# Filler products in TensorE's foreseen stops, layer norms on GpSimd, later issues behind transfers, and new planning tables in a decoder layer

## The chip, the core and the metric

The kernel runs on one core of a Trainium2 chip. A core has five engines, each with its own queue of instructions: TensorE (PE in the profile; its weight loads are PEld), VectorE (DVE), ScalarE (ACT), GpSimd (POOL) and SyncE (SP), which issues the DMA transfers here. Engines wait for one another by semaphores. The metric is device time in microseconds: 1229.28 as the median of three runs of the kernel before (1228.77 to 1231.69).

## The reference

A decoder layer on x of shape (4, 1024, 256), fp32, with three residual blocks: causal self-attention with 16 heads of 16 channels, cross-attention to a context of 77 rows, and a gated feed-forward network with integer weights. Each block begins with a layer norm without weights:

```python
def _layernorm(x, axis=-1, eps=1e-05):
    m = jnp.mean(x, axis=axis, keepdims=True)
    v = jnp.var(x, axis=axis, keepdims=True)
    return (x - m) / jnp.sqrt(v + eps)

x = x + _L0_attn_ref(_layernorm(x), Wq, bq, Wk, bk, Wv, bv, Wo, bo, W_cross, shift_weights, gate)
x = x + _L0_xattn_ref(_layernorm(x), ctx, ctx, mask, xWq, xWk, xWv, xWo)
x = x + _L0_ffn_ref(_layernorm(x), w_gate, w_up, w_down)
```

In the self-attention the scores are `(gt * q W_cross k + (1 - gt) * q (M k)) / 4` with M built from `shift_weights`, then a causal softmax; both score terms are products of q with a mixed k, so their mixing can be folded into the projection weights. In the cross-attention `scores = where(masked, -1e9, scores)` before the softmax. The feed-forward block is `silu(x @ wg.T) * (x @ wu.T) @ wd.T` with 768 hidden channels and weights that are integers from -127 to 127 divided by 127.

## The kernel before

The rows are cut into eight chunks of 512, chunk (b, n) being half n of batch b; on chip a chunk is four tiles of 128 rows by 256 columns (QT = 4). Each chunk goes through these parts:

- `project` (L781): load x, layer norm, eight transposes to xnT, then the k, q and v projections. A projected q or k is split into a high and a low part (`spread`), and transfers (L738) spread the heads over partitions; the scores can start when these have landed.
- `maxima` (L838): scores once, query rows on partitions (L866, and L874 for the causal mask), whose row maxima VectorE takes out of PSUM (mt, L879). `shift` (L747) transposes them.
- `attend` (L907): scores again with keys on partitions (L949), minus the maxima by a product with the selection matrix `sel` (L955), the causal mask (L962), exp on ScalarE (L968) and the product with v (L992). Ahead of its first scores it loads x once more (L919) and GpSimd adds the output bias (L922). It ends with the quotients (L679) and `out_proj` (L698: product L717, addition to x on VectorE L722).
- `cross_attention` (L1052): layer norm, transposes, q projection (L766) and its spreading transfers, a mask product (L1106), scores for the maxima (L1114), their maxima (L1120), the scores again (L1160), exp (L1162), product with v (L1173), `out_proj`.
- `ffn` (L1182): stores x (L1200), layer norm, transposes, a high and a low part of the normalised rows (xh L1207, xl L1209), six hidden chunks of 128 (products L1229; tanh L1235, gating on VectorE L1237, hT L1239 on ScalarE and L1240 on GpSimd), the down products (L1263), the addition to x on VectorE (L1269) and the store (L1272).
- two further parts, `late_weights` and `load_ffn`, prepare the cross-attention's and the feed-forward's weights in the first part of the run. The first of them makes `sel` and `selB` and then sets the flag "selections".

A layer norm is `row_scales` (statistics of four tiles on VectorE, L153 and L154; variance plus epsilon, L156; its power -1/2 on GpSimd, L158; for cross-attention a factor per row, L160) and `normal_rows` (L163; four operations `(x - mean) * scale` of 128 x 256 on VectorE, L166). `layer_norm` calls both. There are 24 in all: 8 each for `project` (the tiles xr; the first chunk's is x00), `cross_attention` and `ffn` (the tiles xn).

**Who sets the order.** Each part is a Python generator. Before it writes instructions it yields a `piece`: the time that they will take on TensorE, the buffers that they take, the earliest start, and the times of what follows on other engines (`use`). All parts run as streams beside one another, and `weave` (L468) picks, while the kernel is built, the stream whose next piece can start first by the planner's own account of engines, buffers and transfers. To a stream's start it adds a number from the table LATES (L1290), one per stream and chunk, which lets a part go earlier or later than the account alone would. The outcome is a fixed order of TensorE's instructions; VectorE's is fixed in the same way up to the flag "begun", and after it the orders of the other engines follow from a scheduler that gives each engine its instructions by the order in which the data come. If the account has TensorE idle for over REST = 1.3 us (L496), it counts what follows for COLD = 5.0 us at a lower rate. These numbers only plan: what an instruction waits for are semaphores.

**Buffers.** PSUM tiles come from `pair()` (three of two banks) and `single()` (two of one bank), L82 to L89; SBUF tiles from rings: w4 (six, for x, xn, xnT, xh, xl), es (six), f2 (six), q, k, v, and x (three). A tile that is asked for waits for the last reader of the buffer that it gets.

Of the kernel before, what the change touches and what calls it, by code (L numbers as in the profile page):

```python
# [8 lines left out]
F32 = mybir.dt.float32  # L9
# [5 lines left out]
ALU = mybir.AluOpType  # L15
# [4 lines left out]
P = 128  # L20
# [7 lines left out]
def tile_decoder_layer(  # L28
# [25 lines left out]
    nc = tc.nc  # L54

    B, S, D = x.shape
# [6 lines left out]
    NG = H // 4  # L63
# [18 lines left out]
    pp = ctx.enter_context(tc.tile_pool(name="pp", bufs=3, space=PSUM))  # L82
    ps = ctx.enter_context(tc.tile_pool(name="ps", bufs=2, space=PSUM))

    def pair():
        return pp.tile([P, 2, CH], F32, tag="pair", name="pair")

    def single():
        return ps.tile([P, CH], F32, tag="single", name="single")  # L89


    ident = const.tile([P, P], F32, name="ident")
# [46 lines left out]
    def x_rows(b, n):  # L139
        xt = wide([P, QT, D], "xr")  # L140
        nc.sync.dma_start(xt, x[b, n * CH : (n + 1) * CH, :].rearrange("(t p) d -> p t d", p=P))
        return xt
# [17 lines left out]
            nc.gpsimd.tensor_tensor(rs, rs, keep, ALU.mult)  # L160
        return mv, rs

    def normal_rows(xt, mv, rs, xn=None):  # L163
        xn = xt if xn is None else xn
        for i in range(QT):
            nc.vector.tensor_scalar(  # L166
                xn[:, i, :], xt[:, i, :], mv[:, i, 0:1], rs[:, i : i + 1],
                ALU.subtract, ALU.mult,
            )
        return xn  # L170
# [133 lines left out]
    first = row_scales(x00)  # L304
    bvx = stage.tile([P, NC, P], F32, name="bvx")
    nc.vector.tensor_copy(bvx, bvn.unsqueeze(2).to_broadcast([P, NC, P]))
    normal_rows(x00, *first)

    def transposed(src, n, put):

# [150 lines left out]
    def piece(pe, use=(), at=0.0, cond=None, free=(), mode="whole", **take):  # L461

        return dict(pe=pe, use=use, at=at, cond=cond, free=free, mode=mode, take=take)

    def weave(*streams, until=None):
        while True:  # L468
            live = [s for s in streams if s.next is not None]
            if not live or until in flags:  # L470
                return
            can = []
            for s in live:
                p = s.next
                if p["cond"] is not None and not p["cond"]():
                    continue
                t = max(
                    tensor["end"], p["at"], *(slots[k].when(c) for k, c in p["take"].items()), 0.0
                )
                if p["pe"] and p["mode"] != tensor["mode"]:  # L480
                    t += SWITCH
                if p["use"] and p["take"]:

                    eng, us = p["use"][0]
                    t = max(t, busy[eng].start(t + p["pe"], us) - p["pe"] - 1.0)
                if t < 1.0e8:
                    can.append((t + (s.lates[s.chunk] if s.lates else 0.0), t, s))
            assert can, [s.next for s in live]
            soon = min(c[0] for c in can) + WAIT
            _, t, s = next(c for c in can if c[0] <= soon)  # L490
            p = s.next
            s.got = {k: [slots[k].take() for _ in range(c)] for k, c in p["take"].items()}
            s.end = t + p["pe"]
            if p["pe"]:
                if t - tensor["end"] > REST:
                    tensor["slow"] = t + COLD  # L496
                s.end += min(max(tensor["slow"] - t, 0.0) / 2, p["pe"])
                tensor.update(end=s.end, mode=p["mode"])
            for token in p["free"]:
                give(token, s.end)  # L500
            s.done = s.end
            for eng, us in p["use"]:
                s.done = busy[eng].run(s.done + LATE, us)
            s.next = next(s.pieces, None)
# [188 lines left out]

        return rest

    NORM = [("DVE", 2.6), ("POOL", 1.1), ("DVE", 1.7)]

    def out_proj(st, nat, t_nat, w, xt):  # L698

# [80 lines left out]
    def project(st, b, n):  # L780

        if (b, n) == (0, 0):
            yield piece(0.0, w4=1)
            xnT, t_x, at = x00T, st.got["w4"], 0.0
        else:
            yield piece(
                0.0, use=[("DMA", 4.0)] * (b > 0) + NORM, w4=1,
                cond=lambda: (("half", b - 1) if b else ("projected", 0, 0, 0)) in flags,
            )
            t_xn = st.got["w4"]  # L790
            xn = x01 if (b, n) == (0, 1) else x_rows(b, n)
            normal_rows(xn, *row_scales(xn))
            flags.add(("normal", b, n))
            yield piece(
                1.1, use=[("ACT", 1.05)], at=st.done + LATE, pair=1, w4=1, free=t_xn
            )
            xnT = transpose_rows(xn)
            st.release("pair")
            t_x = st.got["w4"]
            at = st.done + LATE  # L800
# [102 lines left out]
    def attend(st, b, n):  # L903
# [6 lines left out]
        for g in range(NG):  # L910
            c = g // 2
            if g % 2 == 0:
                yield piece(0.0, cond=lambda: (b, n, c) in shifts and (b, n) in vT and "selections" in flags)
                ms, at, t_ms = shifts.pop((b, n, c))
                if g == 0:
                    yield piece(0.0, x=1, use=[("DMA", 4.0)])
                    xt = xpool.tile([P, QT, D], F32, tag="x", name="x", bufs=3)
                    xs[b, n] = xt, st.got["x"][0]
                    nc.sync.dma_start(  # L919
                        xt, x[b, n * CH : (n + 1) * CH, :].rearrange("(t p) d -> p t d", p=P)  # L920
                    )
                    nc.gpsimd.tensor_tensor(  # L922
                        xt, xt, bo_b.unsqueeze(1).to_broadcast([P, QT, D]), ALU.add
                    )
                q, t_q, _ = qT.pop((b, n, c))
                over = [t_ms, t_q]
                if n == NQ - 1:
                    over += [kT[b, m, c][1] for m in range(NQ)]
            acc = []
            for kb in range(nk):  # L930
# [70 lines left out]
                lag.append(weigh)  # L1001
                if len(lag) > 1:
                    yield from lag.pop(0)()
                if tails and kb == 1:
                    nat, t_nat = yield from quotients(st, tails.pop(), nat, t_nat)
        yield from lag.pop()()
        nat, t_nat = yield from quotients(st, tails.pop(), nat, t_nat)
        yield from out_proj(st, nat, t_nat, woT, xt)
        flags.add(("attended", b, n))

    def quotients(st, tail, nat, t_nat):
        rest, toks, at, g = tail
        yield piece(
            0.55, use=[("DVE", 0.75)], at=at, single=1, free=toks,
            **({"w4": 1} if nat is None else {}),
        )
        if nat is None:
            nat, t_nat = wide([P, QT, D], "nat"), st.got["w4"][0]
        rest(nat, g)
        st.release("single")  # L1020
        return nat, t_nat
# [257 lines left out]
    def every(part, lates, chunks=range(NQ)):  # L1279
# [8 lines left out]
        return Stream(pieces, lates)  # L1288

    LATES = (  # L1290
        [0.00, 0.00, 0.00, 0.00, -0.03, 0.00, -0.31, 0.00],
        [0.00, 0.00, 0.00, 0.00, 0.00, 0.00, -0.23, 0.00],
        [0.00, 0.00, 0.00, 0.00, 0.00, 0.00, 0.00, 0.00],
        [-1.02, 0.03, 0.00, -0.48],
        [0.54, 0.47, 0.00, 0.31],
        [-0.20, -0.15, -0.42, -0.02, 0.00, 0.33, 0.00, 0.00],
    )
    streams = [
        every(maxima, LATES[0]), every(cross_attention, LATES[1]), every(attend, LATES[2]),
# [67 lines left out]
```

## Time and profile before

| what | before |
|---|---|
| median of three runs | 1229.28 us |
| the profiled execution | 1232.86 us |
| its span, first to last instruction | 1231.1 us |
| TensorE busy (mean granted clock) | 1110.8 us (0.958 of full) |
| VectorE busy | 729.9 us |
| ScalarE busy | 562.6 us |
| GpSimd busy | 130.8 us |
| transfers | 76.44 MB, mean 62 GB/s |

The span is counted from the first to the last instruction of one execution; some 1.8 us of that execution lie outside it. A line of the waits gives for TensorE's waiting instruction the engine and the line that released it, and then the total in us, the times, the longest. A line of the timeline gives the start in us, the busy time of a run of like instructions, engine, line, operation, what is written from what, the shape and the number of them, and in brackets how long the engine had been idle and who ended it. A line of the instruction groups gives the count, the busy time in us, the mean in ns, and the idle time of the engine before it. A busy TensorE is not one at full rate: the row PEclk tells the clock that was granted.

### The profile page before, as it was taken

To read this page: it belongs to the slowest core of one execution; us is meant where nothing else is said; L and a number is where in the kernel's file an instruction comes from. 1 tells how busy PE (TensorE), PEld (TensorE's weight loads), DVE (VectorE), ACT (ScalarE), POOL (GpSimd) and SP (SyncE) were. 2 spreads that over 40 slices of the span, in tenths; PEclk is the share of its full clock that TensorE was granted. 3 is DMA by queue.
4 is the path that set the end of the run, shared out by engine and by line. 5 is a ranking of instruction groups with operands and counts; after the bars stand their busy time and mean duration, and the time that the engine had idled before them with its cause. 6 is when DMAs were issued, how large, how long until landed. Compare 5 with 4: busy or idle time off the path is not lost. (4 is left out here: it accounts for less than half of the span.)

```text
span 1231.1 us, 22029 instructions
## 1 busy us (share of the span) xinstructions
PE 1110.8 (90%) x9059; PEld 684.9 (56%) x9059; DVE 729.9 (59%) x1247; ACT 562.6 (46%) x801; POOL 130.8 (11%) x138
## 2 busy tenths in 40 slices
PE   6679989999999898999898998999999889996875
PEld 4445544557555466557555456556575545565654
DVE  5566786354687856255777856347458666136342
ACT  3044544654434463753353563653535336661521
POOL 4031000002000012001100002000110000011212
PEclk9798999999999999999999998999999989998986
DMA  6992315537732016555533015444826140006000
GB/s 124 130 201 63 58 33 69 69 53 92 97 55 40 9 38 110 75 71 87 87 52 38 8 42 70 85 63 60 102 44 91 36 63 8 18 1 86 1 35 19
DMA packets 65438, 76.44 MB, mean 62 GB/s; under 512 B 22451, under 2 KB 39399, under 8 KB 65332
## 3 DMA queue, kind: packets, MB, share of 16 engines
q1 hardware_dynamic: 64227, 74.62, 39.1%
q8 instruction: 73, 1.20, 0.5%
q10 hardware_dynamic: 1104, 0.35, 0.1%
q14 instruction: 34, 0.27, 0.1%
HBM read 15.28 MB, written 9.33 MB: 20 GB/s over the span
## 5 line engine op out<-in xcount | busy, mean ns | idle before, releaser
L968 ACT ACTIVATE es<-pair 128x1024 f32<-128x1024 f32 (+3 forms) x384 | 300.8, 812 | 252.6 <-PE pair L962 178.4
L879 DVE TENSOR_REDUCE mt<-pair 128x2 f32<-128x1024 f32 (+3 forms) x384 | 351.4, 952 | 92.3 <-PE pair L874 60.8
L866 PE MATMUL pair<-k,q 64*128 64x512 f32 (+3 forms) x768 | 163.2, 428 | 29.8 <-DVE mt L879 12.6
L949 PE MATMUL pair<-q,k 64*128 64x512 f32 (+3 forms) x768 | 161.4, 417 | 22.4 <-DVE mt L879 16.5
L992 PE MATMUL single<-es,vs 128*32 128x512 f32 (+3 forms) x1536 | 166.2, 506 | 0.1
L866 PEld LDWEIGHTS pair<-k,q 64*128 64x128 f32 x768 | 76.0, 188 | 121.4 <-DVE mt L879 41.7
L955 PE MATMUL pair<-ms,sel 64*128 64x512 f32 (+3 forms) x768 | 134.6, 347 | 0.0
L949 PEld LDWEIGHTS pair<-q,k 64*128 64x128 f32 x768 | 73.2, 187 | 102.6 <-issue 34.8
L1240 POOL TENSOR_TENSOR hT<-h,hT 128x512 fp32r<-128x512 f32 x48 | 61.4, 1280 | 306.8 <-ACT hT L1239 297.2
L1162 ACT ACTIVATE es<-pair 77x1024 f32<-77x1024 f32 x64 | 63.4, 1020 | 45.8 <-PE pair L1160 45.5
L955 PEld LDWEIGHTS pair<-ms,sel 64*128 64x128 f32 x768 | 74.2, 190 | 3.1
L1120 DVE TENSOR_REDUCE mx<-pair 128x8 f32<-128x616 f32 x64 | 48.7, 794 | 43.7 <-PE pair L1114 43.7
L1263 PE MATMUL pair<-wdT,hT 128*128 128x256 f32 x384 | 63.3, 320 | 11.6 <-POOL hT L1240 4.8
L158 POOL TENSOR_TENSOR rs<-ve,mhalf 128x4 f32<-128x4 f32 x24 | 24.3, 1012 | 439.5 <-DVE ve L156 439.4
L1235 ACT ACTIVATE h<-pair 128x512 f32<-128x512 f32 x48 | 28.7, 598 | 89.0 <-PE pair L1229 84.8
L874 PE MATMUL pair<-cm_qk,id 64*128 64x64 bf16 (+1 forms) x1024 | 69.0, 211 | 0.0
L962 PE MATMUL pair<-cm_kq,id 64*128 64x64 bf16 (+1 forms) x1024 | 67.3, 211 | 0.0
L1236 DVE SCALAR_TENSOR_TENSOR h<-h,pair 128x512 f32<-128x512 f32 x48 | 33.0, 687 | 57.5 <-ACT h L1235 57.2
L1263 PEld LDWEIGHTS pair<-wdT,hT 128*128 128x128 f32 x384 | 55.8, 216 | 18.4 <-POOL hT L1240 6.3
L1114 PE MATMUL pair<-k2s,q 128*128 128x156 f32 x256 | 46.7, 308 | 12.1 <-DMA q<-hi 5.3
L992 PEld LDWEIGHTS single<-es,vs 128*32 128x32 f32 x1536 | 32.4, 109 | 40.7 <-issue 29.6
L674 ACT COPY aS<-single 128x512 f32<-128x512 f32 x64 | 37.5, 589 | 31.6 <-PE single L992 19.0
(180 smaller groups left out, 1575.0 us busy)
## 6 DMA issues: line engine op xcount, KB each, us to landing
q<-hi SPq DMA_DIRECT2D x128, 128.0 KB, 5.1
q<-lo SPq DMA_DIRECT2D x128, 128.0 KB, 6.3
k<-hi SPq DMA_DIRECT2D x64, 128.0 KB, 4.3
k<-lo SPq DMA_DIRECT2D x64, 128.0 KB, 6.0
xr<-in_x_dram SPq DMA_DIRECT2D x8, 512.0 KB, 6.0
x<-in_x_dram SPq DMA_DIRECT2D x8, 512.0 KB, 7.4
x_dram<-x SPq DMA_DIRECT2D x8, 512.0 KB, 2.6
out_dram<-x SPq DMA_DIRECT2D x8, 512.0 KB, 3.7
```

The lines of the kernel that those rows point to most:

```text
L866: nc.tensor.matmul(t[:, j, :w], q[r, a, i * P : (i + 1) * P], k[r, a, :w], start=True, stop=True,)
L874: nc.tensor.matmul(t[:, j, w - P + 64 * half : w], id2[r, half], cm_qk[r, half, 64 * half :], start=False, stop=True, skip_group_check=True,)
L879: nc.vector.tensor_reduce(mt[:, i, :, p, kc], t[:, :, :w], AX.X, ALU.max)
L949: nc.tensor.matmul(t[:, j, lo:], k[r, a, ki * P : (ki + 1) * P], q[r, a, lo:], start=True, stop=False,)
L955: nc.tensor.matmul(t[:, j, lo:], sel[r, hp, :], ms[r, lo:], start=False, stop=True)
L962: nc.tensor.matmul(t[:, j, lo : lo + 64 * (half + 1)], id2[r, half], cm_kq[r, half, : 64 * (half + 1)], start=False, stop=True, skip_group ...
L968: nc.scalar.activation(es[:, :, lo:], t[:, :, lo:], AF.Exp)
L992: nc.tensor.matmul(acc[0][W * jj : W * (jj + 1), lo:], vs[:, ki, V1 * h : V1 * h + W], both[jj // 2][:, jj % 2, lo:], start=(kb == 0), sto ...
L1120: nc.vector.tensor_reduce(mt[:, i, h4 : h4 + 4, :].rearrange("q (k p) j -> q k (p j)", k=2), tv[:, :, :, :S2], AX.X, ALU.max,)
L1162: nc.scalar.activation(es[:S2], t[:S2], AF.Exp)
L1240: nc.gpsimd.tensor_tensor(hs[:, 1, :], h, hs[:, 0, :].bitcast(F32), ALU.subtract)
L1263: nc.tensor.matmul(t[:, i, :], h[1][:, v, i * P : (i + 1) * P], w[:, h[0], :], start=(m == 0), stop=(m == len(terms) - 1),)
```

## The change

1. *Filler products.* In `weave`, where a piece of TensorE would start over REST after the last one ended, and a PSUM buffer for it is free early, and `sel` exists, the idle time less 0.7 us is noted (`stand`). The next `pair()` or `single()` then first writes so many products of 512 columns (one per 0.235 us of it) into the tile that it hands out, from `selB` and `sel`. Nothing reads what they write: the products that follow begin with `start=True`. Where fillers are noted the planner doesn't count the slow rate.
2. *Norms on GpSimd.* `normal_rows` runs on GpSimd, but for the first chunk's x00. The planner's price of a norm (`NORM`) becomes 2.4 us of VectorE and then 3.4 of GpSimd.
3. *Later issues.* In `project` the load of x has a piece of its own, and the norm's instructions are issued in a second piece whose earliest start is the load's end by the account. In `attend` the load of x moves from ahead of the first scores to the last group's first block, and GpSimd's addition of the bias to a piece behind the last product with v. The account prices either transfer at 6.5 us (4.0 before).
4. *Tables.* The six rows of LATES (maxima, cross-attention, attend, project of the first and of the second half of a batch, ffn) have new entries.

```diff
--- before.py
+++ after.py
@@ -82,11 +82,23 @@
     pp = ctx.enter_context(tc.tile_pool(name="pp", bufs=3, space=PSUM))
     ps = ctx.enter_context(tc.tile_pool(name="ps", bufs=2, space=PSUM))
 
+
+
+    stand = {"us": 0.0}
+
+    def stirred(t, part):
+        for _ in range(int(stand["us"] / 0.235)):
+            nc.tensor.matmul(part, selB, sel[:, 0:4, :], start=True, stop=True)
+        stand["us"] = 0.0
+        return t
+
     def pair():
-        return pp.tile([P, 2, CH], F32, tag="pair", name="pair")
+        t = pp.tile([P, 2, CH], F32, tag="pair", name="pair")
+        return stirred(t, t[:, 0, :])
 
     def single():
-        return ps.tile([P, CH], F32, tag="single", name="single")
+        t = ps.tile([P, CH], F32, tag="single", name="single")
+        return stirred(t, t)
 
 
     ident = const.tile([P, P], F32, name="ident")
@@ -160,10 +172,10 @@
             nc.gpsimd.tensor_tensor(rs, rs, keep, ALU.mult)
         return mv, rs
 
-    def normal_rows(xt, mv, rs, xn=None):
+    def normal_rows(xt, mv, rs, xn=None, eng=nc.gpsimd):
         xn = xt if xn is None else xn
         for i in range(QT):
-            nc.vector.tensor_scalar(
+            eng.tensor_scalar(
                 xn[:, i, :], xt[:, i, :], mv[:, i, 0:1], rs[:, i : i + 1],
                 ALU.subtract, ALU.mult,
             )
@@ -304,7 +316,7 @@
     first = row_scales(x00)
     bvx = stage.tile([P, NC, P], F32, name="bvx")
     nc.vector.tensor_copy(bvx, bvn.unsqueeze(2).to_broadcast([P, NC, P]))
-    normal_rows(x00, *first)
+    normal_rows(x00, *first, eng=nc.vector)
 
     def transposed(src, n, put):
 
@@ -492,7 +504,11 @@
             s.got = {k: [slots[k].take() for _ in range(c)] for k, c in p["take"].items()}
             s.end = t + p["pe"]
             if p["pe"]:
-                if t - tensor["end"] > REST:
+                idle = t - tensor["end"]
+                early = max([slots[k].when(1) for k in ("pair", "single") if k in p["take"]] or [t])
+                if idle > REST and early < tensor["end"] + 0.5 and "selections" in flags:
+                    stand["us"] = idle - 0.7
+                elif idle > REST:
                     tensor["slow"] = t + COLD
                 s.end += min(max(tensor["slow"] - t, 0.0) / 2, p["pe"])
                 tensor.update(end=s.end, mode=p["mode"])
@@ -693,7 +709,7 @@
 
         return rest
 
-    NORM = [("DVE", 2.6), ("POOL", 1.1), ("DVE", 1.7)]
+    NORM = [("DVE", 2.4), ("POOL", 3.4)]
 
     def out_proj(st, nat, t_nat, w, xt):
 
@@ -784,11 +800,12 @@
             xnT, t_x, at = x00T, st.got["w4"], 0.0
         else:
             yield piece(
-                0.0, use=[("DMA", 4.0)] * (b > 0) + NORM, w4=1,
+                0.0, use=[("DMA", 6.5)] * (b > 0), w4=1,
                 cond=lambda: (("half", b - 1) if b else ("projected", 0, 0, 0)) in flags,
             )
             t_xn = st.got["w4"]
-            xn = x01 if (b, n) == (0, 1) else x_rows(b, n)
+            xn = x_rows(b, n) if b else x01
+            yield piece(0.0, use=NORM, at=st.done)
             normal_rows(xn, *row_scales(xn))
             flags.add(("normal", b, n))
             yield piece(
@@ -912,16 +929,6 @@
             if g % 2 == 0:
                 yield piece(0.0, cond=lambda: (b, n, c) in shifts and (b, n) in vT and "selections" in flags)
                 ms, at, t_ms = shifts.pop((b, n, c))
-                if g == 0:
-                    yield piece(0.0, x=1, use=[("DMA", 4.0)])
-                    xt = xpool.tile([P, QT, D], F32, tag="x", name="x", bufs=3)
-                    xs[b, n] = xt, st.got["x"][0]
-                    nc.sync.dma_start(
-                        xt, x[b, n * CH : (n + 1) * CH, :].rearrange("(t p) d -> p t d", p=P)
-                    )
-                    nc.gpsimd.tensor_tensor(
-                        xt, xt, bo_b.unsqueeze(1).to_broadcast([P, QT, D]), ALU.add
-                    )
                 q, t_q, _ = qT.pop((b, n, c))
                 over = [t_ms, t_q]
                 if n == NQ - 1:
@@ -1001,9 +1008,19 @@
                 lag.append(weigh)
                 if len(lag) > 1:
                     yield from lag.pop(0)()
+                if g == NG - 1 and kb == 0:
+                    yield piece(0.0, x=1, use=[("DMA", 6.5)])
+                    xt = xpool.tile([P, QT, D], F32, tag="x", name="x", bufs=3)
+                    xs[b, n] = xt, st.got["x"][0]
+                    nc.sync.dma_start(
+                        xt, x[b, n * CH : (n + 1) * CH, :].rearrange("(t p) d -> p t d", p=P)
+                    )
+                    x_at = st.done
                 if tails and kb == 1:
                     nat, t_nat = yield from quotients(st, tails.pop(), nat, t_nat)
         yield from lag.pop()()
+        yield piece(0.0, use=[("POOL", 1.5)], at=x_at)
+        nc.gpsimd.tensor_tensor(xt, xt, bo_b.unsqueeze(1).to_broadcast([P, QT, D]), ALU.add)
         nat, t_nat = yield from quotients(st, tails.pop(), nat, t_nat)
         yield from out_proj(st, nat, t_nat, woT, xt)
         flags.add(("attended", b, n))
@@ -1288,12 +1305,12 @@
         return Stream(pieces, lates)
 
     LATES = (
-        [0.00, 0.00, 0.00, 0.00, -0.03, 0.00, -0.31, 0.00],
-        [0.00, 0.00, 0.00, 0.00, 0.00, 0.00, -0.23, 0.00],
         [0.00, 0.00, 0.00, 0.00, 0.00, 0.00, 0.00, 0.00],
-        [-1.02, 0.03, 0.00, -0.48],
-        [0.54, 0.47, 0.00, 0.31],
-        [-0.20, -0.15, -0.42, -0.02, 0.00, 0.33, 0.00, 0.00],
+        [0.00, -0.03, -0.10, 0.00, 0.00, -0.04, 0.01, -0.57],
+        [0.02, 0.00, 0.00, 0.00, 0.03, 0.00, 0.00, 0.00],
+        [0.43, -0.03, 0.06, -0.10],
+        [0.61, 0.21, 0.14, 0.21],
+        [0.00, -0.30, 0.00, -0.14, 0.08, 0.32, -0.26, 3.69],
     )
     streams = [
         every(maxima, LATES[0]), every(cross_attention, LATES[1]), every(attend, LATES[2]),
```

## The prediction

> **What bounds the kernel now.** I began with the page's slices of the span: the busy tenths of TensorE and the tenths of full clock that it was granted, 31 us a digit.
>
> ```profile
> PE   6679989999999898999898998999999889996875
> PEclk9798999999999999999999998999999989998986
> ```
>
> TensorE is the bound: busy 1110.8 of 1231.1 us, VectorE 729.9, ScalarE 562.6, GpSimd 130.8. Its 120.3 us of idleness lie in the first 60 us (some 25), in the tail from 1110 us (about 34) and in scattered stops between (about 57). Clock digits under 9 stand in the same places: after a long stop products run at half rate for a while. So an edit can win only a TensorE stop, or the half-rate stretch behind one. Next the waits of TensorE, by what ended them (us in total, times, longest):
>
> ```profile
> PE pair L949 <- DVE mt L879: 16.5, 22, 3.8
> PE pair L866 <- DVE mt L879: 12.6, 16, 3.2
> ...
> PE pair L182 <- DVE xn L166: 6.1, 2, 4.9
> PE pair L1114 <- DMA q<-hi: 5.3, 1, 5.3
> ```
>
> Three kinds matter: VectorE's maxima (mt) that release a pair buffer late; the transfers that spread a cross-attention q; the last layer norms. One stop of each, from the timeline (start, busy us, idle before in brackets):
>
> ```profile
> 480.25 0.64 PE L1114 MATMUL pair<-k2s,q 128*128 128x156 f32 x4 [2.60 <-DMA q<-lo]
> ...
> 763.01 1.11 PE L1114 MATMUL pair<-k2s,q 128*128 128x156 f32 x4 [2.94 <-issue]
> ...
> 984.47 2.34 POOL L922 TENSOR_TENSOR x<-x,bo_b 128x1024 f32<-128x1024 f32 x1
> 984.55 3.38 DVE L166 TENSOR_SCALAR xn<-x,mv,rs 128x256 f32<-128x256 f32 x4 [0.95 <-POOL rs L160]
> ...
> 988.59 0.79 PE L949 MATMUL pair<-q,k 64*128 64x512 f32 x2 [3.80 <-DVE mt L879]
> ...
> 1126.23 1.11 PE L1114 MATMUL pair<-k2s,q 128*128 128x156 f32 x4 [5.33 <-DMA q<-hi]
> ...
> 1187.03 1.94 PE L182 MATMUL pair<-ident,xn 128*128 128x128 f32 x8 [4.93 <-DVE xn L166]
> ...
> 1219.20 0.47 PE L1263 MATMUL pair<-wdT,hT 128*128 128x256 f32 x1 [2.60 <-ACT hT L1239]
> 1220.60 3.14 PE L1263 MATMUL pair<-wdT,hT 128*128 128x256 f32 x13 [0.93 <-POOLq L1320]
> ```
>
> At 984.55 four norms take 3.38 us on VectorE, stretched beside GpSimd's add, and two maxima (L879) stand behind them until 989.1: TensorE stops 3.80 us. At 480, 763 and 1126 TensorE has issued all its other work and waits for q. At 1187 and 1219 it waits on the last chunk's own chain. A 512-column product starts every 0.233 us at full rate; from 1191.92 they start 0.43 apart.
>
> **What the Trainium skill says.** "TensorE: Matmul & The Clock Gate", Part 1: The HAM clock gate, says that an idle array drops to half rate and needs about 3.4 us of activity to come back, counted in a free-running window. The trace agrees: after 5.33 us idle, half rate from 1126.2 to 1130.4; after 4.93, from 1187 to 1195.3 with further short stops in it. "SBUF — State Buffer", Who interferes with whom, says that VectorE and GpSimd share one port pair as an exclusive lock, which a reduction of VectorE does not take. The trace agrees for norms: four took 1.38 us alone at 1186.47 and 3.38 beside L922.
>
> **The change, part by part.** Sums are made against the profiled 1232.9 us (span 1231.1 plus 1.8 around it); the median of the runs is 1229.3, 3.6 less, so I take the difference from there.
>
> *Price of a norm on GpSimd.* No row shows one. 23 norms of four operations move (L166, all but x00's): about 44.7 us leave VectorE (27.0 + 19.1 - 1.4). GpSimd's one-input rows with a change of type bound it below:
>
> ```profile
> L641 POOL CAST wi<-wi 128x1024 f32<-128x1024 int32 x2 | 2.1, 1038 | 13.6 <-DMA wi<-in_L_ffn_w_gate_dram 13.0 <-DMA wi<-in_L_ffn_w_up_dram 0.6
> ...
> L641 POOL CAST wi<-wi 128x512 f32<-128x512 int32 x2 | 1.2, 616 | 17.2 <-DMA wi<-in_L_ffn_w_gate_dram 13.9 <-PE single L588 3.3
> ```
>
> The slope is 0.82 ns a column, so 256 columns cost 616 - 256 x 0.82 = 0.41 us; from its two-input rows (1280 ns for 512 columns in L1240, 2368 for 1024 in L922: 2.12 a column) 1280 - 256 x 2.12 = 0.74. I take 0.55, 2.2 us a norm against 1.4 to 3.4 on VectorE. Range kept: 0.41 to 0.74, and 1.2 or more for the case that scalars from memory are slow there. GpSimd is 89% idle, so its 51 us hide; the chain of a norm grows by up to 0.8.
>
> *Fillers.* In the order after, 93 products of 512 columns stand in seven places, all in the tail: 19 and 8 ahead of the last chunk's two cross-attention halves (L1114), 6 ahead of its last shift, 4 ahead of a down group (L1263), 29 ahead of the last norm's transposes, 9 ahead of the first hidden product, 18 ahead of the last down group. At 0.235 us they fill 21.9 us that are idle anyhow, at 0.43 they would take 40. They win the half rate behind a stop, and nothing of the stop itself.
>
> *The tail, from 1093 us to the end.* (a) Four more L1229 products (0.93 us) stand ahead of the last chunk's norm transposes and what follows lands about 2.0 earlier, since the second half of q is projected and spread sooner: -2.0. (b) Behind the first filled stop five scores run 0.24 instead of 0.43 (-1.0), and eight transposes (1.7 at half rate, 0.9 at full) fill the 1.08 us wait before L1160: -2.3 in all. (c) Five waits of 0.7 to 0.8 between 1144 and 1182 are partly covered by L1229 products put there: -1.8. (d) A group of 16 L1263 (2.0 us) moves from before the last L717 to behind it, into the norm's wait: -2.0. (e) The last norm: before, from L717's end at 1182.1, transposes started after 4.9 us and the second hidden chunk ended after 14.7. After, an add L1269 (1.2) stands among the statistics, the norm is done at +8.5, 29 fillers end at +8.7, transposes at +9.5, nine fillers at +11.6, products at full rate, end +15.35: +0.65. (f) At the end 18 fillers (4.2) cover 2.60 + 0.93, then 13 L1263 run 0.117 apart instead of 0.22: -1.2. Sum -8.6. The half-rate stretches from 1203.7 and 1213 (2.4 us together) get no filler and stay.
>
> *q transfers of cross-attention.* Cover is the other TensorE work between the q projection and its first L1114. Before, chunks with 8.1, 8.1, 6.8 and 5.9 us waited 2.60, 2.94, 5.33 and 1.26; all from 11.4 up waited nothing: 10.7 to 11 is needed. After, the two middle ones have 11.2 and 13.3: -2.6 and -2.9, and with them the half rate behind (482 to 485.3, 761.8 to 768.6; half of each, -1.7 and -3.4). At most -10.6; I take -8, since a cover of 11.2 is near the need.
>
> *VectorE's norms ahead of maxima.* The stops of 3.80 (988.59) and 1.85 (198.31) go when no norm stands on VectorE, and 6.9 and 3.4 us of half rate behind them, half of which is lost time: 5.65 + 5.15 = -10.8 at most; other maxima are as late as before. I take -7.5.
>
> *What is late next.* The new order of all middle work puts VectorE denser where batch 2 is projected: over some 80 us its work is 1.05 of TensorE's, 0.98 before: 80 x 0.05 = +4. TensorE work between an L717's end and the norm's transposes is 6.6, 6.6, 8.2, 8.4, 8.4, 8.8 us in six places, 9.1 up elsewhere; the need is 5.4 + 2.2 + 0.2 = 7.8, so two short stops, +2. *Moved loads:* x and its add L922 go behind the last scores, and the add stands on GpSimd behind no norm of its chunk; xr's transfer is issued before, its norm when it has landed, so that no engine queue holds a wait for it: nothing, with 0.5 us a chunk (+4) if the add is late. *The start:* the second q projection moves behind eight maxima, and its spreading transfers stand on SP behind some 1.8 MB of weight loads, one of which waits for VectorE; against that the stop of 3.19 us at 91.8 and its half rate (to 99.6) may go. -7 to +5; I take 0 with the moved loads.
>
> Sum: -8.6 - 8 - 7.5 + 4 + 2 = -18. 1229.3 - 18 = 1211.
>
> **Rivals.** *A, as worked out* (0.55): 1211, own range 1202 to 1219. *B, only the tail gains* (0.23): the middle's order is new everywhere and its stops merely move, as 29 us of waits for maxima in 38 places suggest; against it, the two covers have grown: 1229.3 - 8.6 = 1221. *C, slower: GpSimd is too slow at the norm* (0.14). At p us an operation the need is 5.6 + 4p. At p = 1.2 it is 10.4: the six places above stop 3.8 + 3.8 + 2.2 + 2.0 + 2.0 + 1.6 = 15.4, others about 1, the last norm, on the path whole, (1.2 - 0.55) x 4 = 2.6, together 19, or 17 more than the sum above holds: about the 18 won. At 1.5 (need 11.6) 22.6 + about 6 + 3.8 - 2 = 30: 1211 + 30 = 1241. For it: an operation there with two scalars from memory isn't in the trace, and pow on 4 columns takes 1.01 us; against it, casts at 0.82 ns a column. *D, fillers do not keep the clock* (0.08): if they run cold at 0.43, 93 of them overrun their stops by 40 - 21.9 = 18: 1229, no change. Against it, a real product of that shape warms the array at 1195.3.
>
> **How the numbers follow.** The likeliest is A: 1211. The range reaches from A with the upper gains (10.6, 10.8 and 5 at the start instead of 8, 7.5 and 0: 1200, a little more for the tail's waits: 1196) to D's end: 1229; outside lie most of C and some of A's low end, 0.17. About 3.7 us (0.3%) is what a measurement can tell from no change. Faster: A, B but its top, and some of D, 0.80; same 0.06; slower 0.14.
>
> **What would show it.** Right: norms on GpSimd at 0.4 to 0.75 us; VectorE near 685 busy; no stop over 1 us before L1114 in the middle; no stop of 3.8 behind a norm; clock over 0.97 with full digits at the end; fillers at 0.235. Wrong: norms above 1 us; waits of L182 for a GpSimd xn in many places; longer totals of waits for mt; TensorE filling its stops past the moment when what it waits for has come.

## The result, and the profile after

The changed kernel takes 1251.95 us (median of four runs, 1248.23 to 1252.61) against 1229.03 for the kernel before on the same chip: a ratio of 1.0175, 95% interval 1.0151 to 1.0200. It is some 22 us slower; the prediction was 1211. The profiled execution has a span of 1250.8 us, with TensorE busy 1127.5 (23 of it fillers), VectorE 693.3, GpSimd 242.2, and a granted clock of 0.967 (0.958 before).

The slices of the page of the changed kernel, busy tenths and granted clock:

```profile
PE   6689889998899998999989999999798989998996
...
PEclk9699999999999999999889999999999999999998
```

Half of the story of the prediction is there. The clock digits of the tail, which ended 9998986 before, are 9s but for the last, and the half rate at 762 to 769 us is gone. But a busy digit of 7 stands at 875 us, and the clock falls at 595 to 655 us. Counted in windows from 100 to 1100 us, TensorE is idle 74.9 us after and 56.8 before. Line numbers below are those of the changed kernel: the norm's operation is L178 (L166 before), its transposes L194 (L182), the scores for maxima L883 (L866) and their reduction L896 (L879), h L1252 to L1254 (L1235 to L1237), hT on GpSimd L1257 (L1240), the down products L1280 (L1263), fillers L91.

The groups by form of GpSimd in the changed kernel (busy us, mean ns, idle before):

```profile
L178 POOL TENSOR_SCALAR xn<-x,mv,rs 128x256 f32<-128x256 f32 x64 | 77.3, 1221 | 1.7
L1257 POOL TENSOR_TENSOR hT<-h,hT 128x512 fp32r<-128x512 f32 x48 | 61.2, 1278 | 268.9 <-ACT hT L1256 241.5 <-issue 20.8 <-PE pair L1246 4.3
L178 POOL TENSOR_SCALAR xr<-xr,mv,rs 128x256 f32<-128x256 f32 x28 | 33.9, 1222 | 0.7
```

An operation of the norm takes 1.22 us on GpSimd, not 0.55. All 92 take 1.217 to 1.228 us, whatever runs beside them, so waiting behind VectorE is not what makes them long. Four take 4.9 us, where VectorE took 1.4 to 3.4. The Trainium skill's "GPSIMD Engine Reference", 4.1 Engine selection, calls operations with one input roughly line-rate there; this case disagrees for this form (0.40 us on VectorE undisturbed), and the measurement decides. Its section 3.1, Elementwise, has 4497 ns for a sum of two inputs of 2048 columns on GpSimd; an eighth of that, as an estimate for 256 columns, is 0.56 us. A product of two inputs did take 0.61 us (e4 below), so that figure fits its own form and is half of what the norm's takes.

The waits of TensorE after (us in total, times, longest):

```profile
PE pair L883 <- DVE mt L896: 14.1, 25, 2.3
PE pair L956 <- DVE mt L896: 12.2, 21, 1.9
...
PE pair L194 <- POOL xn L178: 8.4, 14, 0.8
...
PE pair L883 <- DVE h L1254: 6.6, 4, 1.8
PE pair L194 <- DVE h L1254: 5.8, 2, 3.7
```

The stops of 3.8 us behind a maximum are gone, as forecast, and L1131 (L1114 before) has no stop over 1 us behind q but in the tail. In their place stand transposes waiting for a GpSimd norm, and a wait that was small before: a pair buffer that h releases late. The timeline shows how that second one arises:

```profile
294.54 4.83 POOL L178 TENSOR_SCALAR xn<-x,mv,rs 128x256 f32<-128x256 f32 x4
...
299.33 1.26 POOL L1257 TENSOR_TENSOR hT<-h,hT 128x512 fp32r<-128x512 f32 x1
300.63 0.60 ACT L1252 ACTIVATE h<-pair 128x512 f32<-128x512 f32 x1 [7.02 <-POOL hT L1257]
...
301.26 0.69 DVE L1253 SCALAR_TENSOR_TENSOR h<-h,pair 128x512 f32<-128x512 f32 x1 [4.68 <-ACT h L1252]
...
301.98 0.69 DVE L1254 TENSOR_TENSOR h<-h,pair 128x512 f32<-128x512 f32 x1
...
302.82 1.06 PE L194 MATMUL pair<-ident,xn 128*128 128x128 f32 x8 [2.13 <-DVE h L1254]
```

Read it from the top. The feed-forward's hT stands behind the 4.83 us of a norm on GpSimd's queue. Until hT has read its h, ScalarE may not write the h that gets the same SBUF buffer (7.02 us of waiting), so VectorE's gating is late, so the PSUM pair that it reads stays taken, and TensorE stops for want of a buffer, at a product that has nothing to do with the feed-forward. The waits of ScalarE sum it up, first in the kernel before and then in the changed one:

```profile
ACT h L1235 <- POOL hT L1240: 4.2, 3, 1.4
...
ACT h L1252 <- POOL hT L1257: 16.8, 4, 7.0
```

In the tail the fillers did what was planned. From the timeline of TensorE near the end:

```profile
1204.82 6.76 PE L91 MATMUL pair<-sel,selB 128*128 128x512 f32 x29
1211.42 0.60 PE L194 MATMUL pair<-ident,xn 128*128 128x128 f32 x4
1212.37 0.44 PE L194 MATMUL pair<-ident,xn 128*128 128x128 f32 x2 [0.34 <-POOL xn L178]
1213.57 0.44 PE L194 MATMUL pair<-ident,xn 128*128 128x128 f32 x2 [0.76 <-POOL xn L178]
...
1237.77 4.29 PE L91 MATMUL pair<-sel,selB 128*128 128x512 f32 x18
1241.90 2.07 PE L1280 MATMUL pair<-wdT,hT 128*128 128x256 f32 x16
```

29 fillers start 0.23 us apart and end at 1211.6, and the transposes run at the full rate as each tile arrives, every 1.2 us: GpSimd's pace. The last 16 down products take 2.07 us instead of 3.14 for 13.

### The profile page after: what moved, and what is told of

Read it like the earlier page. It is cut to its first block, busy times and chain, and to the rows that moved or that the text cites. A ratio compares the mean times of both kernels' runs of the same rounds, so it can differ in the third digit from the quotient of the medians.

```text
span 1250.8 us, 22275 instructions
## 1 busy us (share of the span) xinstructions
PE 1127.5 (90%) x9152; PEld 699.9 (56%) x9152; DVE 693.3 (55%) x1155; ACT 562.9 (45%) x801; POOL 242.2 (19%) x230
## 4 chain that ended last, share of the span: by engine, by line
PE 37%; DVE 9%; issue 6%; POOL 6%; DMA 4%; ACT 3%; SPq 1%; POOLq 0%; ACTq 0%; DVEq 0%
PE single L999 5%; DVE mt L896 4%; PE pair L956 4%; PE single L782 3%; PE pair L883 3%; PE pair L1246 3%; POOL xn L178 3%; PE pair L1280 2%; PE pair L733 2%; PE pair L962 2%; DMA q<-lo 2%; PE pair L1177 2%; PE single L1190 2%; PE pair L194 1%; PE single L695 1%
## 5 line engine op out<-in xcount | busy, mean ns | idle before, releaser
L896 DVE TENSOR_REDUCE mt<-pair 128x2 f32<-128x1024 f32 (+3 forms) x384 | 351.7, 953 | 109.6 <-PE pair L891 76.2
L883 PE MATMUL pair<-k,q 64*128 64x512 f32 (+3 forms) x768 | 165.2, 433 | 42.8 <-DVE mt L896 14.1
L956 PE MATMUL pair<-q,k 64*128 64x512 f32 (+3 forms) x768 | 161.9, 417 | 16.9 <-DVE mt L896 12.2
L883 PEld LDWEIGHTS pair<-k,q 64*128 64x128 f32 x768 | 78.0, 192 | 129.6 <-DVE mt L896 44.6
L956 PEld LDWEIGHTS pair<-q,k 64*128 64x128 f32 x768 | 73.4, 187 | 97.5 <-issue 40.2
L1257 POOL TENSOR_TENSOR hT<-h,hT 128x512 fp32r<-128x512 f32 x48 | 61.2, 1278 | 268.9 <-ACT hT L1256 241.5
L178 POOL TENSOR_SCALAR xn<-x,mv,rs 128x256 f32<-128x256 f32 x64 | 77.3, 1221 | 1.7
L700 DVE RECIPROCAL rd<-single 128x16 f32<-128x16 f32 x64 | 16.3, 254 | 98.0 <-PE single L695 97.8
L1252 ACT ACTIVATE h<-pair 128x512 f32<-128x512 f32 x48 | 28.7, 597 | 88.7 <-PE pair L1246 71.9
L1280 PE MATMUL pair<-wdT,hT 128*128 128x256 f32 x384 | 57.6, 301 | 7.8 <-POOL hT L1257 4.5
L1280 PEld LDWEIGHTS pair<-wdT,hT 128*128 128x128 f32 x384 | 50.9, 198 | 14.2 <-POOL hT L1257 6.0
```

Source lines behind the costliest of these rows:

```text
L178: eng.tensor_scalar(xn[:, i, :], xt[:, i, :], mv[:, i, 0:1], rs[:, i : i + 1], ALU.subtract, ALU.mult,)
L883: nc.tensor.matmul(t[:, j, :w], q[r, a, i * P : (i + 1) * P], k[r, a, :w], start=True, stop=True,)
L896: nc.vector.tensor_reduce(mt[:, i, :, p, kc], t[:, :, :w], AX.X, ALU.max)
L956: nc.tensor.matmul(t[:, j, lo:], k[r, a, ki * P : (ki + 1) * P], q[r, a, lo:], start=True, stop=False,)
L1257: nc.gpsimd.tensor_tensor(hs[:, 1, :], h, hs[:, 0, :].bitcast(F32), ALU.subtract)
L1280: nc.tensor.matmul(t[:, i, :], h[1][:, v, i * P : (i + 1) * P], w[:, h[0], :], start=(m == 0), stop=(m == len(terms) - 1),)
```

## The experiments

Two theories stood at first. P: the price of a norm on GpSimd turned the gain into a loss, by its longer chain and by what stands behind it on the queue. O: the new order of the middle loses by itself. TensorE's order is the changed kernel's in e1, e4 to e8 and e15, the same without fillers in e14, that of the kernel before in e2, e9 and e13, and in e3 that plus fillers. Each ratio is against the kernel before on the same chip, whose own runs there lie within 1223 to 1238 us.

**e1, norms back on VectorE in the changed order.**

```diff
-    def normal_rows(xt, mv, rs, xn=None, eng=nc.gpsimd):
+    def normal_rows(xt, mv, rs, xn=None, eng=nc.vector):
```

> The changed kernel with its norms on VectorE again; TensorE's order, fillers, later issues and tables are those of the changed kernel. Theory P (a norm on GpSimd costs 1.22 us an operation; its chain is 3 us longer and the feed-forward's hT stands behind 4.8 us of it on GpSimd's queue): the loss goes with the norms, 1215 to 1230 us, and the stops behind L1254 at 296, 302, 316, 882, 888 and 903 us vanish. Theory O (the new order of the middle loses by itself): 1243 or more.

Measured: 1258.77 us, ratio 1.0248 (1.0203 to 1.0293): slower still. P in this plain form falls. The changed order was laid for a VectorE without norms; with them L956 waits up to 5.5 us for a maximum (1.9 after). L883 waits 10.4 us behind h there (6.6 after), although no norm stands on GpSimd.

**e2, the norms alone on GpSimd, in the order of before** (the same edit, made to the kernel before).

> The kernel before with nothing but the 23 norms on GpSimd; TensorE's order is that of before. Theory P: slower by 12 to 30 us, 1241 to 1259, since the order was made for short norms. Theory O: within 5 us of 1229.

Measured: 1245.95 us, ratio 1.0117 (1.0084 to 1.0150). This is what P expects: the norms alone cost 14 us even in the order of before. Two lines of the waits grew most (6.1 and 4.8 us for the like before):

```profile
PE pair L182 <- POOL xn L166: 18.0, 17, 5.7
PE pair L1263 <- POOL hT L1240: 13.5, 8, 4.4
```

The second is the queue again, seen in the timeline of GpSimd and TensorE: three of four operations of a norm, then hT, and 13 down products that waited 4.39 us for it:

```profile
467.27 3.64 POOL L166 TENSOR_SCALAR xr<-xr,mv,rs 128x256 f32<-128x256 f32 x3
...
470.88 1.26 POOL L1240 TENSOR_TENSOR hT<-h,hT 128x512 fp32r<-128x512 f32 x1
...
472.19 2.87 PE L1263 MATMUL pair<-wdT,hT 128*128 128x256 f32 x13 [4.39 <-POOL hT L1240]
```

**e3, fillers alone, in the order of before.** `stand` is set as in the change, the planner's slow rate is kept, so that nothing moves.

> The kernel before with nothing but fillers in its own foreseen stops (104 products in nine places), its order otherwise kept. If fillers win the half rate behind stops: 3 to 7 us faster, 1222 to 1226, mean clock up from 0.958 to about 0.97. If they overrun what they wait for: 1229 or more.

Measured: 1231.23 us, ratio 1.0019 (1.0002 to 1.0036), the second of the two cases. The clock rose to 0.964 in the profiled execution, but the time did not fall, for two reasons. First, 15 of the 104 fillers stand where the plan foresaw a stop and the chip has none. The transposes that started without a wait in the kernel before (first line) now start behind these fillers (second line, L89), some 3.5 us later:

```profile
213.30 1.05 PE L182 MATMUL pair<-ident,xr 128*128 128x128 f32 x8
...
215.11 3.64 PE L89 MATMUL pair<-sel,selB 128*128 128x512 f32 x15
```

In the changed kernel all 93 fillers stand in the tail, so e3 is no measure of them. Second, the 5.3 us behind the first half of the last chunk's q were filled to 1.2. But where a transfer ends the stop, products that arrive sooner only wait longer at the next one: L1128 (L1114 before) then waited 3.34 us for the second half instead of 1.26, and the totals of that wait read

```profile
PE pair L1128 <- DMA q<-lo: 7.9, 3, 3.3
```

against 3.9 before.

**e4, the price of the forms.** Each GpSimd norm does its four tiles in four forms (the code is shortened).

```diff
+            if eng is nc.vector or i == 0: eng.tensor_scalar(xn_i, x_i, mean, rs, subtract, mult)
+            elif i == 1: eng.tensor_scalar(xn_i, x_i, rs, None, mult)
+            elif i == 2: eng.tensor_scalar(xn_i, x_i, 0.125, 0.875, subtract, mult)
+            else: eng.tensor_tensor(xn_i, x_i, rs repeated along the row, mult)
```

> The changed kernel with the four operations of each GpSimd norm in four forms, so the output is not normalised: subtract and multiply with two scalars from memory; multiply alone with one; subtract and multiply with two constants; a two-input product with a scale repeated along the row. If the two scalars from memory cost the time: 1.22, about 0.8, about 0.4, 0.74 us. If GpSimd's loop over two arithmetic steps costs it: 1.22, 0.8, 1.2, 0.74.

The groups of this kernel's GpSimd by form:

```profile
L179 POOL TENSOR_SCALAR xn<-x,mv,rs 128x256 f32<-128x256 f32 x16 | 19.7, 1229 | 1.7
...
L188 POOL TENSOR_SCALAR xn<-x 128x256 f32<-128x256 f32 x16 | 17.4, 1085 | 321.6 <-DVE x L751 321.3
L184 POOL TENSOR_SCALAR xn<-x,rs 128x256 f32<-128x256 f32 x16 | 14.9, 933 | 0.0
L192 POOL TENSOR_TENSOR xn<-x,rs 128x256 f32<-128x256 f32 x16 | 9.8, 614 | 0.0
```

Constants in place of the two scalars from memory save 0.14 us, and a single step with one scalar is still 0.93. Neither expectation held whole: neither the scalars' place nor the second step explains most of it. The form `tensor_scalar` is slow in all three kinds, and a product of two inputs, which does as much arithmetic as the third line, takes two thirds of that line's time. A single execution of the whole kernel, with norms of 3.9 us, took 1229.39 us. That lies within e5's range below, whose norms take 2.5, so most of the loss may set in only between 3.9 and 4.9 us; one execution doesn't settle it.

**e5, the changed kernel at about the planned price.** All four tiles in the fourth form, 2.5 us a norm (the plan has 3.4 for it with the 1.2 of the scales). The mean is left out.

> The changed kernel with each GpSimd norm operation as one product with the row's scale (0.61 us each in the run before, 2.5 us a norm instead of 4.9); the mean is not subtracted there, so the output is not the layer's. TensorE's order is that of the changed kernel. Theory P (the price of a norm on GpSimd alone turned the gain into a loss): 1206 to 1218, near the sum of the prediction, and faster than before. Theory Q (the price is part of it, and the new order loses too): 1222 or more.

Measured: 1228.03 us (1219.64 to 1232.20), ratio 0.9974 (0.9956 to 0.9992). Against 1.0175 that is 0.0201 x 1229 = 24.7 us, the worth of the real price in this order. But it wins 3 us where the prediction's sum has 18: the order loses too (theory Q).

**e6, half on each engine**: `(nc.vector if i % 2 else eng).tensor_scalar(...)`.

> The changed kernel with two tiles of each norm on GpSimd and two on VectorE, beside one another: 2.4 us on GpSimd, 0.8 to 1.7 on VectorE. The result is the layer's. Theory P: most of what the cheap norm wins, 1212 to 1225. If VectorE's relief from norms is what the new order needs: 1230 or more, toward the 1259 of the norms on VectorE.

Measured: 1253.69 us, ratio 1.0204 (1.0139 to 1.0270), the second case. GpSimd's share is short, but half of VectorE's relief is gone (L956 waits up to 4.1 us for a maximum, 1.9 in the changed kernel), and nothing is won over the changed kernel.

**e7, norms on ScalarE**: `nc.scalar.activation(xn_i, x_i, Identity, scale=rs_i, bias=nb_i)`, with nb = -mean x rs from VectorE.

> The changed kernel with the norms on ScalarE as scale and offset in one operation (one small VectorE operation makes the offset). The result is the layer's up to rounding. If ScalarE has room where norms fall and takes 0.4 to 0.5 us an operation: 1208 to 1222, below both kernels. If exps stand in the way and es come late: 1235 or more.

Measured: 1280.97 us, ratio 1.0416 (1.0365 to 1.0466). An operation takes 0.59 us, but the exps queue behind it. The waits of TensorE for the scores' buffers rise from 7.0 and 1.0 us to

```profile
PE pair L892 <- ACT es L984: 11.1, 11, 4.1
...
PE pair L965 <- ACT es L984: 10.4, 9, 2.3
```

These are 13.5 of the some 30 us that separate it from the changed kernel; where the others come from stays open.

**e8, hT on VectorE**: the subtraction of L1257 as `nc.vector.tensor_tensor`, norms on GpSimd as in the change.

> The changed kernel with the feed-forward's low part hT on VectorE, so that it no longer stands behind a norm on GpSimd's queue. If that queue is the larger half of the loss: 1235 or less, and no stops of 1.5 us and more behind h at 296, 302, 882 and 888 us. If 48 more operations on VectorE (about 0.7 us each, 33 us) cost as much: 1245 to 1260.

Measured: 1237.67 us, ratio 1.0070 (1.0047 to 1.0093). That is between the two cases: 12.9 us are won back (0.0105 x 1229) although VectorE does 33.5 us of subtractions more. Not all of it is the price's, since the same move wins 2.7 us with the cheap norm (e15 below). So the queue behind the norm is some 10 of the price's 24.7 us, uncertain by 5; the other 14.5 are there with hT on VectorE too (e8 against e15, 0.0118 x 1229). The stop of 3.7 us at 888 is gone in it; the total of L883 behind h stayed (6.2 against 6.6), so not all of those stops are GpSimd's.

**e9, two places alone.** The kernel before, with the norms of batch 1's rows on GpSimd and every other tile of the cross-attention norm of chunk (3, 0); only the lines that choose the places are shown.

```diff
-            normal_rows(xn, *row_scales(xn))
+            normal_rows(xn, *row_scales(xn), engs=(nc.gpsimd if b == 1 else nc.vector,) * 2)
-        xn = layer_norm(xt, keep[:, it])
+        xn = layer_norm(xt, keep[:, it], (nc.gpsimd if (b, n) == (3, 0) else nc.vector, nc.vector))
```

> The kernel before, TensorE's order kept, with GpSimd doing only the two norms of batch 1's rows ahead of their projection (the reductions at 189 to 199 us wait for them on VectorE) and two of four tiles in the cross-attention norm at 984 us. In the run with all norms on GpSimd these two places won 3.1 and 5.4 us. If the gain stays where no chain gets longer: 1221 to 1226, below both kernels. If it is given back at the next stop: within 3 us of before.

Measured: 1222.68 us, ratio 0.9961 (0.9945 to 0.9978), below both kernels: the first case. The stop of 3.80 us of the prediction's timeline has become

```profile
978.82 0.49 PE L949 MATMUL pair<-q,k 64*128 64x512 f32 x2 [1.31 <-DVE mt L879]
```

and no half-rate stretch follows it.

**e10 to e12, other inputs to the plan.** e10: the kernel before with the new tables. e11: with the later issues and their prices. e12: the changed kernel with the plan told ("POOL", 6.2) instead of 3.4.

> The kernel before with the new LATES tables alone. The tables belong to a plan with short VectorE norms. If the new order of the middle is by itself no worse: within 6 us of 1229. If the tables are what gives the middle's gain back: 1236 or more.

> The kernel before with the later issues alone (loads priced 6.5 us, the norm's instructions in a piece of their own behind the load, x and its bias addition at the end of the attention). The prediction's step: 0, to +4 if the addition comes late; so 1225 to 1234, with the plan's order shifted by the prices.

> The changed kernel with the plan told what a GpSimd norm takes (6.2 us with the scales, in the place of 3.4), so TensorE's order is made for it; the tables are as they are. If the loss comes from an order that expects norms too early: 1232 to 1244. If a norm of 4.9 us on GpSimd costs as much in any order, by its chain and by hT behind it: 1246 or more.

Measured: 1272.50 us (ratio 1.0362, 1.0344 to 1.0380), 1353.47 (1.1014, 1.0988 to 1.1040) and 1332.51 (1.0845, 1.0825 to 1.0864). e10 and e12 are in the second of their two cases, e12 far beyond what its reason would give, and e11 is far above its one range. In each of them TensorE's order is another one throughout, and no single stop explains the time: in e11 two waits of 12.3 and 9.3 us stand out,

```profile
PE single L747 <- DVE mpad L888: 14.5, 3, 12.3
PE single L679 <- ACT aS L674: 13.8, 8, 9.3
```

of 124 us. What they show is that a table serves the prices that it was made with: the old pair gives 1229, the new pair with cheap norms and no fillers 1231 (e14), mixtures 1272 to 1353. What the later issues cost in an order made for them can't be read from e11, and stays open. e12 doesn't tell either whether an order could absorb norms of 4.9 us; it tells that the plan needs new tables when it gets a new price.

**e13 to e15, what the cheap norm shows.** e13: the order of before, all norms on GpSimd in the cheap form. e14: e5 without fillers. e15: e5 with hT on VectorE. The mean is left out in all three.

> The kernel before, TensorE's order kept, with all 23 norms on GpSimd in the cheap form (the product with the row's scale alone, 2.5 us a norm; the mean is left out). If norms off VectorE win what the prediction took (-7.5) and chains of 2.5 us cost little: 1219 to 1224. If chains longer by 1 us and hT behind 2.5 us give it back: 1226 to 1232.

> The changed kernel with cheap norms (mean left out) and none of the 93 fillers, the order otherwise that of the changed kernel. If fillers win the half rate in the tail, about 2 us by the prediction's sum: 1229 to 1232, against 1228 with them. If they give back by overrun what they win: 1226 to 1229.

> The changed kernel with cheap norms (mean left out) and hT on VectorE. If the stops of 1.6 to 1.9 us behind h in the middle (at 300, 317, 436, 864, 881 us) are GpSimd's queue: they go, and the time falls to 1216 to 1223. If they come from the order of the feed-forward's products itself: they stay, and 1228 to 1236.

Measured: e13 1220.09 us, ratio 0.9911 (0.9878 to 0.9944); e14 1231.11, 1.0005 (0.9979 to 1.0032); e15 1225.37, 0.9952 (0.9932 to 0.9972). e13 and e14 ran on one chip and differ only in what makes the new order (tables, prices, later issues). Both are in the first of their two cases. The waits of e13, TensorE behind hT, q and h, where L1268 is the down product and L954 a score:

```profile
PE pair L1268 <- POOL hT L1245: 9.1, 7, 2.4
...
PE pair L1119 <- DMA q<-hi: 5.3, 1, 5.3
...
PE pair L954 <- DVE h L1242: 1.2, 1, 1.2
```

and of e14, where L888 and L1285 are a score and the down product:

```profile
PE pair L888 <- DVE h L1259: 6.9, 4, 1.8
PE pair L888 <- ACT es L980: 6.7, 10, 1.1
...
PE pair L1285 <- DVE h L1259: 2.2, 2, 1.9
```

From 100 to 1100 us TensorE is idle 51.7 us in e13 and 65.2 in e14 (62.8 in e5). Behind h it waits 9.9 us in e14 (the two lines above and 0.8 elsewhere), 2.2 in e13 (1.0 elsewhere); and with hT on VectorE (e15) that wait is still 6.8 for L888, the second case in the stops, though the time lies between the two. So these stops are not GpSimd's queue at this price but the order's: the timeline has two or three hidden chunks (eight products of L1251 each) in one run there, and behind them products that need a pair buffer at once. From the last L717 of the self-attention to the end of the span, however, e14 takes 124.3 us and e13 129.3: the new order of the tail is better, by 5.0.

## Why the prediction was wrong, point by point

Put together from the ratios, times 1229 us, the change comes apart like this:

| part | from | us |
|---|---|---|
| norms off VectorE at 2.5 us each, old order | e13 | -10.9 |
| the new order (tables, prices, later issues) | e14 - e13 | +11.6 |
| fillers in that order | e5 - e14 | -3.8 |
| the norm's real price, 4.9 us | after - e5 | +24.7 |
| sum | | +21.6 |

Each difference is uncertain by some 4 to 5 us; the signs of all but the fillers' are clear of that. For the fillers the traces agree: from the last L717 of the self-attention to the end, 124.3 us without them (e14), 119.8 and 120.2 with them (e5, e15).

**The step that failed first is the price of a norm on GpSimd**, "I take 0.55", with 0.41 to 0.74 kept as its range. It measured 1.22. A cast and a two-input product were taken as bounds from below and above, but neither has the form of the operation, and e4 shows that the form decides: a two-input product of the same size is at half the price. The plan of the changed kernel has the same figure (3.4 less 1.2 of scales, over four: 0.55); agreement with it was no evidence. Two of the signs that the prediction named for being wrong are there: norms above 1 us, and transposes that wait for a GpSimd norm in many places (18 times for L194).

**Rival C named half of this mechanism.** At 1.2 us an operation it has 17 us for the longer chain, which puts the measured price at 1229. With hT off GpSimd the price costs 14.5 us (e8 against e15), and TensorE's transposes wait 12.4 us for GpSimd norms in e8, 0.9 in e15. In e8:

```profile
PE pair L194 <- POOL xn L178: 8.9, 14, 0.8
...
PE pair L194 <- POOL xr L178: 3.5, 4, 1.2
```

That part of C is borne out. It left out the queue: "GpSimd is 89% idle, so its 51 us hide" speaks of totals, where what counts is that hT comes from the same engine, in the same stretch, while another chunk's norm stands there. That is the other 10 us or so. And C took the rest of the sum, -18, as won; e5 has -3.

**Norms ahead of maxima, -7.5: right.** In e13, instruction by instruction against the kernel before, the two stops named (198 and 988 us) and the slow stretch behind them win 2.8 and 4.9 us, together 7.7; in e9 it is 2.7 and 4.3, and 4.8 in the medians (uncertain by 2).

**q transfers, -8: right where it looked.** In the changed kernel no stop over 1 us before L1131 is behind q until the tail, and in e5 the clock from 450 to 500 and from 750 to 800 us is 1.00 (0.97 and 0.93 before). What this wins by itself was not measured: these covers come with the new order, which as a whole loses.

**The tail, -8.6: right in size at the planned price.** From the last L717 of the self-attention to the span's end the kernel before takes 129.2 us and e5 119.8, -9.4. About half of it is the order's (e13 129.3, e14 124.3) and half the fillers' (e14 against e5). In the changed kernel it is 126.8, because the two norms there stand on the path at 4.9 us. Of step (e): the fillers ended at +9.2 after L717's end (+8.7 forecast), the norm at +11.1 (+8.5), the transposes at +11.6 (+9.5).

**What is late next, +4 and +2: too small, and in the wrong place.** VectorE's density was looked at, and the cover of norms. The order's own new stops lie elsewhere: pair buffers that h holds, 9.9 us where there were 2.2, part of 13.5 us more idleness in the middle. This is the second step that failed: for the new order with its fillers the sum has -10.6 (-8.6 - 8 + 4 + 2), and they measured +7.8 (11.6 - 3.8). Where the rest of the idleness comes from was not traced. The start and the moved loads, put at 0, are in these 11.6 and were not measured alone. e10 to e12 show how far an order can go wrong, and that nothing in the diff's small numbers tells it. Rival B, the middle gives its gain back, is nearest to what e5 found, and e5 went further: 1228 where B has 1221.

**Rival D fell**: fillers ran at 0.23 us and kept the clock. Their worth is small all the same: -3.8 us in the changed order, uncertain by 4. The +2.3 of e3 holds some 3.5 us of fillers where there was no stop; besides, a stop that a transfer ends is not shortened by arriving earlier.

The forecast's signs, 0.80 for faster, rested on a price without a row. C, with a chance of 0.14, was left mostly outside a range that ended at 1229.

## What to carry to other kernels

When work moves to an engine that is mostly idle, price the operation by a row of its own form, or measure it alone first; then list what else comes from that engine in the same stretch, and follow the buffers that this work holds: here a subtraction behind a norm held an SBUF tile, which held a PSUM pair, which stopped TensorE. A planner's tables belong to its prices; a change of either is a new order that has to be measured as a whole. And of a relief that costs something everywhere, take only the places where it pays: two whole norms and half of a third gave a kernel 0.4% faster than the one before, while all 23 gave one that is slower by 1.2%.

## What the hardware showed unasked

On GpSimd a `tensor_scalar` of 128 x 256 took 1.22 us with two scalars from memory, 1.09 with two constants, 0.93 with one step, and a `tensor_tensor` with a repeated column 0.61. On ScalarE scale and offset of the same tile took 0.59 us, on VectorE 0.40 undisturbed. The half rate of TensorE comes not only behind long stops: in e14 stops of 1.01 and 0.78 us at 611 and two of 0.84 and 1.52 at 637 to 640 were followed by clocks of 0.74 and 0.71 in the next 10 us windows, while in e5, in the same order and behind stops of the same length, the first was followed by 1.00 and at the second the clock was 0.83. The Trainium skill's "TensorE: Matmul & The Clock Gate", Part 1: The HAM clock gate, calls the window in which activity is counted free-running. That fits, since the same stops can then fall into it differently; no run here shows the window itself. The clock goes with the time: executions of e5 spread from 1219.6 us at a mean of 0.981 to 1232.2 us at 0.970.
